# Two stages of a software pipeline, each cut in two: the divisors of the attention contexts and the running products of the cosines

## The chip, the cores and the metric

The kernel runs on one core of one Trainium2 chip. The time is device microseconds (us) of one launch, taken as the median of several runs. The times of single instructions come from the trace of one profiled execution.

## What is computed

Four layers work on four images of 128 channels and 64 x 64 pixels. A state-space layer and a convolution come first (layers 0 and 1), then an attention with a small feed-forward (layer 2), an expert layer, a linear attention, and an expert layer again. The change lies in layer 2. There an image is 4096 tokens of 128 numbers, in 16 heads of 8; the queries, keys and values of a head are one and the same tensor, made of running products of cosines:

```python
def _qz_ring(phi):
    c = jnp.cos(phi)
    P = jnp.cumprod(c, axis=-1)
    z0 = jnp.prod(c[..., 1:], axis=-1, keepdims=True)
    return jnp.concatenate([z0, P[..., 1:]], axis=-1)
...
qkv = _qz_ring(heads + rx_theta)
...
attn = jax.nn.softmax(scores, axis=-1)
ctx = jnp.einsum('bhst,bhtd->bhsd', attn, q)
...
x1 = _ln(x + attn_out, g1, beta1)
zf = jnp.cos(x1[..., :NQ_FFN]) * jnp.cos(ry_theta)
h = jax.nn.relu(zf @ w1.T + b1)
ffn_out = h @ w2.T + b2
return _ln(x1 + ffn_out, g2, beta2)
```

The input of the layer is a layernorm of the tokens, and its answer is added to them.

## The kernel before

Layer 2 (`layer2_attention`, L825) takes the images one after another, in a loop over `b` at L1312 that runs five times. Each pass has two stretches. In the first one, `prepare` of image `b` (L914) and `feed_forward` of image `b - 1` (L1227) run side by side; in the second, `attention` of image `b` runs (L1003). So the first pass holds preparation alone, the next three hold both (called joint stretches here), and the fifth holds feed-forward alone. The attention has the order of PE, DVE and POOL written out by hand (`manual_schedule`) and is not touched.

An image is cut into eight chunks of 512 tokens. A stage is a function of the chunk's number `c`, and `in_turn` (L797) makes a pipeline of stages: in turn `i` it calls stage `k` for chunk `i - k`, the last stage first. `run` (L820) takes the steps of several such pipelines by turns, one call of each. What these calls record is not yet the order on the engines. Outside the attention a scheduler of the compiler takes all recorded instructions, with their dependencies and buffers, and lays them out engine by engine, in an order that depends on its own estimate of when each can start. On the chip each engine then works through its list in order, and an instruction that has to wait holds up all behind it on that engine. Loads and stores are issued on SP, in order as well.

Preparation has five stages. `fetch` loads the chunk (`x_in`). `centred` subtracts the mean on PE (`ln_xc`) and squares on ACT (`ln_sq`). `norm` makes the variance on PE (`ln_var`), the inverse root on DVE and ACT (L110 to L115) and the normed chunk on DVE (`nrm`, L118), which is stored. `products` turns the chunk to tokens on PE (`tok_t`, L943), adds the angle on DVE (`phi`, L945), and takes the cosine, `K.cos` (L196): the multiple of two pi on DVE and ACT (`cos_k`, L200 and L201), the rest on DVE (`cos_r`, L203 and L204), the absolute value and the sine on ACT (L205, L206), each sine after a table load where the last table was that of the square root. The result is `cs`. Still in `products`, POOL multiplies the cosines 1 to 7 (`q0`, one L955 and five L957), DVE makes seven running products in place (L959), the first of which overwrites what POOL reads, and DVE copies `q0` into place 0 (L960). `store` copies `cs` to the values on ACT (L965), every second time starts four stores of them, turns it on PE (`q_t`, L980), copies that (`tq`, ACT), splits it in two parts on DVE and POOL (`rest`, `part`, L984 to L987) and stores these as heads (L988). At the end the first head's keys and queries are loaded back (L903, 32 loads) and rounded on POOL (L912).

Feed-forward has nine stages. `fetch` loads the two halves of the contexts (`num`, two buffers), the sums of their weights (`den`) and the normed chunk (`nrm_in`). `attended` turns the sums on PE (`den_t`, L1246), adds them up and takes the reciprocal on DVE (L1248 to L1250), copies it for the 8 numbers of each head (`rc`, L1252), turns it back on PE (`rd_ps`), adds the halves on POOL (L1256), divides on DVE (L1257), multiplies with a weight on PE (`att_ps`) and adds to the normed chunk on DVE (L1260). Then come `first_centred` and `first_norm` (a layernorm that ends on POOL, L121), `cosines` (`z_ps`, then `K.cos` as `zf`), `hidden` (`hid_ps`, four relus on ACT), `sum_up` (`ffn_ps`, L1295), `last_centred`, and `last_norm`, which adds to the tokens on POOL (L1306) and stores them (L1307).

PE is the matrix engine, DVE the vector engine, ACT the engine of activations, POOL the general one, SP the queue of loads and stores.

Of the kernel before, what the change touches and what calls it, by code (L numbers as in the profile page):

```python
# [9 lines left out]
F32 = mybir.dt.float32  # L10
# [7 lines left out]
P = 128  # L18
# [4 lines left out]
NCH = L // CH  # L23
# [773 lines left out]
def in_turn(n, *stages):  # L797


    for i in range(n + len(stages) - 1):  # L800
        for k in reversed(range(len(stages))):
            if 0 <= i - k < n:
                stages[k](i - k)
                yield
# [20 lines left out]
def layer2_attention(K, xd, dpool, w):  # L825

    nc, tc, mm = K.nc, K.tc, K.mm
    NH, HD = 16, 8
# [3 lines left out]
    with ExitStack() as ctx:  # L832
# [77 lines left out]
        def rounded(t):  # L910

            nc.gpsimd.tensor_copy(t, t.bitcast(F32))  # L912

        def prepare(b, big, two, work, psum):  # L914

            n = NTT * NH * (HD + 1)
            qt = big.tile([P, n + 32], F32, name="qt")
            nc.gpsimd.memset(qt[:, n:], 0.0)  # L920
            values = qt[:, 0:n].rearrange("p (h t d) -> p t h d", h=NH, d=HD + 1)
            nc.gpsimd.memset(values[:, :, :, HD : HD + 1], 1.0)
            shape = [P, 4, NH, HD]
            heads, xs, nrms, laters, halves = {}, {}, {}, {}, {}

            def fetch(c):
                xs[c] = work.tile([P, CH], F32, name="x_in", bufs=3)
                nc.sync.dma_start(out=xs[c], in_=xd[b][:, c * CH : (c + 1) * CH])

            def centred(c):  # L930
                nrms[c] = work.tile([P, CH], F32, name="nrm", bufs=3)
                halves[c] = K.layernorm_steps(nrms[c], xs.pop(c), work, psum, tag="xc", bufs=3)
                next(halves[c])

            def norm(c):
                next(halves.pop(c), None)
                nc.sync.dma_start(out=nrm_d[b % 2][:, c * CH : (c + 1) * CH], in_=nrms[c])

            def products(c):

                tp = psum.tile([P, 4, P], F32, name="tok_t", tag="mm")
                for j in range(4):
                    nc.tensor.transpose(tp[:, j, :], nrms[c][:, j * P : (j + 1) * P], K.ident)  # L943
                phi = work.tile(shape, F32, name="phi")
                nc.vector.tensor_tensor(  # L945
                    phi.rearrange("p t h d -> p (t h) d"),
                    tp.rearrange("p j (h d) -> p (j h) d", d=HD),
                    theta.unsqueeze(1).to_broadcast([P, 4 * NH, HD]),
                    ALU.add,
                )  # L950
                cs = heads[c] = work.tile(shape, F32, name="cs", bufs=3)
                K.cos(cs, phi, work, shape, "cos")
                cc = lambda d: cs[:, :, :, d : d + 1].rearrange("p t h o -> p (t h) o")
                q0 = work.tile([P, 4 * NH, 1], F32, name="q0")
                nc.gpsimd.tensor_tensor(q0, cc(1), cc(2), ALU.mult)  # L955
                for d in range(3, HD):
                    nc.gpsimd.tensor_tensor(q0, q0, cc(d), ALU.mult)  # L957
                for d in range(1, HD):
                    nc.vector.tensor_tensor(cc(d), cc(d - 1), cc(d), ALU.mult)  # L959
                nc.vector.tensor_copy(cc(0), q0)  # L960

            def store(c):

                cs = heads[c]
                nc.scalar.copy(values[:, 4 * c : 4 * c + 4, :, 0:HD], cs)  # L965
                j = c // 2
                if c % 2 == 0 and j < NJ - 1:
                    laters[j] = work.tile([P, NH, BT, HD], F32, name="later", bufs=1)
                if j < NJ - 1:
                    at = laters[j][:, :, 4 * (c % 2) : 4 * (c % 2) + 4]  # L970
                    nc.gpsimd.tensor_copy(at.rearrange("p h t d -> p t h d"), cs)
                if c % 2 and j < NJ - 1:
                    for q in range(4):
                        nc.sync.dma_start(
                            out=value_d[:, :, j, q].rearrange("h s t d -> s h (t d)"),
                            in_=laters[j][32 * q : 32 * q + 32].rearrange("s h t d -> s h (t d)"),
                        )
                tp = psum.tile([P, 4, P], F32, name="q_t", tag="mm")
                for j in range(4):
                    nc.tensor.transpose(tp[:, j, :], cs[:, j].rearrange("p h d -> p (h d)"), K.ident)  # L980
                tq = work.tile([P, CH], F32, name="tq", tag="phi")
                nc.scalar.copy(tq, tp.rearrange("p j t -> p (j t)"))
                rest = work.tile([P, CH], F32, name="rest", tag="cos_r")
                nc.vector.scalar_tensor_tensor(rest, tq, 4097.0, tq, ALU.mult, ALU.subtract)  # L984
                part = work.tile([P, 2, CH], F32, name="part")
                nc.vector.scalar_tensor_tensor(part[:, 0], tq, 4097.0, rest, ALU.mult, ALU.subtract)
                nc.gpsimd.tensor_tensor(part[:, 1], tq, part[:, 0], ALU.subtract)  # L987
                nc.sync.dma_start(  # L988
                    out=head_d[:, :, c * CH : (c + 1) * CH].rearrange("z q s -> q z s"), in_=part
                )  # L990

            first = []

            def stages():
                yield from in_turn(NCH, fetch, centred, norm, products, store)
                first.extend(load(0, two))
                for t in first:
                    rounded(t)
                yield

            return stages(), qt, first

        def attention(qt, first, dsum, big, two, work, pssc, psctx, psacc):  # L1003
# [222 lines left out]

        def feed_forward(b, dsum, work, psum):  # L1227

            loads, x1s, hids, sums, halves, lasts = {}, {}, {}, {}, {}, {}

            def fetch(c):
                cols = slice(c * CH, (c + 1) * CH)
# [5 lines left out]
                nc.sync.dma_start(out=nrm, in_=nrm_d[b % 2][:, cols])  # L1238
                loads[c] = num, den, nrm

            def attended(c):
                num, den, at = loads[c]

                tp = psum.tile([P, 4, 2 * NH], F32, name="den_t", tag="mm")
# [3 lines left out]
                nc.vector.tensor_reduce(rd, tp.rearrange("p j (z h) -> p j h z", z=2), AX.X, ALU.add)  # L1248
                nc.vector.tensor_tensor(rd, rd, dsum[:, 4 * c : 4 * c + 4], ALU.add)
                nc.vector.reciprocal(rd, rd)  # L1250
                rc = work.tile([P, 4, NH, HD], F32, name="rc")
                nc.vector.tensor_copy(rc, rd.unsqueeze(3).to_broadcast([P, 4, NH, HD]))  # L1252
                rp = psum.tile([P, 4, P], F32, name="rd_ps", tag="mm")
                for j in range(4):
                    mm(rp[:, j, :], rc[:, j].rearrange("p h d -> p (h d)"), K.ident)
# [46 lines left out]
            def last_norm(c):  # L1302
# [3 lines left out]
                nc.gpsimd.tensor_tensor(x, x, o, ALU.add)  # L1306
                nc.sync.dma_start(out=xd[b][:, c * CH : (c + 1) * CH], in_=x)  # L1307

            return in_turn(NCH, fetch, attended, first_centred, first_norm, cosines, hidden, sum_up, last_centred, last_norm)

        past = None
        for b in range(NB + 1):  # L1312
# [459 lines left out]
```

## Time and profile before

| | us |
|---|---|
| median of 3 runs | 10838.9 (10834.5 to 10853.2) |
| profiled execution | 10849.6 |
| its span, first to last instruction | 10847.5 |
| preparation alone (3204.0 to 3357.8) | 153.8 |
| three joint stretches, last exponential of one image to first of the next | 247.8, 248.7, 249.1 |
| feed-forward alone (9536.7 to 9689.6) | 152.9 |
| busy in the span: PE, DVE, ACT, POOL | 9021, 7648, 7513, 5239 |

The five stretches are some 1052 us of the span; the attention blocks between them take about 1358 us each. In the views below, a line of the timeline has the start in us from the span's start, the duration, the engine, the line of the program, the operation, what it writes and reads with shapes, and in brackets how long the engine stood idle before it and what ended that. A row of the table of busy time has a stretch, its length, and for each engine the busy time and the number of instructions in it. A row of the waits says which engine's operation waited for which, then total, number of times and longest.

### The profile page before, as it was taken

The numbers are of one execution on the slowest core, as the hardware profiler recorded it, in microseconds if no ns is written. First come the engines' busy times: TensorE is split into PE (matmuls) and PEld (weight loads), VectorE is DVE, ScalarE is ACT, GpSimd is POOL, SyncE is SP. The second block draws the span as 40 slices with busy tenths as digits, with TensorE's granted clock in tenths as the row PEclk, the third lists the DMA queues.
The fourth block names the chain that finished last, engine by engine and source line by source line (L and its number), as shares of the span: only waits on it lengthen the run. The fifth ranks groups of instructions, "written<-read, shape, count | busy, mean of one in ns | idle before, by whom it ended". The sixth has DMA issues, their size and how long they took to land. (4 is left out here: it accounts for less than half of the span.)

```text
span 10847.5 us, 184105 instructions
## 1 busy us (share of the span) xinstructions
PE 9021.2 (83%) x71952; PEld 3473.1 (32%) x71952; DVE 7647.7 (71%) x8462; ACT 7513.2 (69%) x10317; POOL 5239.0 (48%) x3143
## 2 busy tenths in 40 slices
PE   5777778777866999978999978999978999976767
PEld 2123323322342333333333333333333333323433
DVE  2787677668856777767777767777767777754563
ACT  2665575565526999967999968999958999942431
POOL 1565555556634655645566635666635665520000
PEclk8788878878878999989999989999989999987888
DMA  3322322321212112222221122222222212223004
GB/s 81 88 70 56 89 73 55 86 75 50 62 60 49 34 33 36 37 68 44 33 38 35 33 71 42 38 35 34 33 75 42 35 34 33 33 89 105 6 17 140
DMA packets 524325, 581.58 MB, mean 54 GB/s; under 512 B 106232, under 2 KB 329536, under 8 KB 520896
## 3 DMA queue, kind: packets, MB, share of 16 engines
q1 hardware_dynamic: 523456, 569.81, 22.9%
q8 instruction: 568, 9.31, 0.4%
q14 instruction: 301, 2.47, 0.1%
HBM read 373.96 MB, written 76.55 MB: 42 GB/s over the span
## 5 line engine op out<-in xcount | busy, mean ns | idle before, releaser
L1208 ACT ACTIVATE ex<-score 128x1024 f32<-128x1024 f32 x5120 | 4934.2, 1033 | 469.8 <-PE score L90 180.1
L90 PE MATMUL ctx_ps<-ex,qt 128*32 128x512 f32 x20480 | 2719.4, 595 | 0.0
L1155 POOL TENSOR_TENSOR folded<-ex 128x1024 f32<-128x1024 f32 x704 | 1679.6, 2386 | 2074.2 <-ACT ex L1208 2054.2
L1214 DVE STREAM_TRANSPOSE turned<-ex 128x1024 f32<-128x1024 f32 x1536 | 1879.5, 1224 | 491.5 <-ACT ex L1208 428.1
L90 PE MATMUL acc_ps<-turned,turned_v 128*32 128x256 f32 x24576 | 1826.2, 388 | 181.4 <-DVE turned L1194 179.6
L1194 DVE STREAM_TRANSPOSE turned<-ex 128x1024 f32<-128x1024 f32 x1536 | 1854.0, 1207 | 0.0
L90 PE MATMUL score<-queries,keys 32*128 32x512 f32 x10240 | 1358.3, 496 | 140.7 <-ACT ex L1208 81.0
L687 DVE TENSOR_TENSOR_SCAN hs<-decay,carry,hs 128x512 f32<-128x512 f32 x1024 | 1252.8, 1266 | 197.3 <-ACT decay L686 183.0
L686 ACT ACTIVATE decay<-dt,a_neg 128x512 f32<-128x512 f32 x1024 | 700.9, 689 | 794.3 <-DVE hs L687 772.6
L90 PEld LDWEIGHTS score<-queries,keys 32*128 32x128 f32 x10240 | 524.3, 182 | 2196.0 <-issue 1666.2
L693 POOL TENSOR_TENSOR hs<-hs,c_sb 128x1024 f32<-128x1024 f32 x512 | 1205.1, 2375 | 43.5 <-DMA c_sb<-c_d 24.0
L1156 POOL TENSOR_TENSOR quarters<-folded 128x512 f32<-128x512 f32 x704 | 905.4, 1286 | 55.2
L90 PEld LDWEIGHTS acc_ps<-turned,turned_v 128*32 128x32 f32 x24576 | 561.6, 108 | 897.8 <-issue 555.8
L90 PEld LDWEIGHTS ctx_ps<-ex,qt 128*32 128x32 f32 x20480 | 684.5, 109 | 461.4 <-DVE ctx L1137 53.1
L90 PE MATMUL y_ps<-hs,pair 128*64 128x512 f32 x2048 | 652.3, 761 | 138.6 <-POOL hs L693 138.5
L683 DVE TENSOR_TENSOR hs<-dtx,b_ps 128x2048 f32<-128x2048 f32 x256 | 582.3, 2275 | 261.8 <-PE b_ps L90 177.1
L1137 DVE COPY ctx<-ctx_ps 128x512 f32<-128x512 f32 x256 | 177.0, 692 | 669.8 <-PE ctx_ps L90 669.8
L690 POOL COPY carry<-hs 128x4 f32<-128x4 f32 x256 | 59.8, 234 | 1028.0 <-DVE hs L687 990.5
L1027 POOL TENSOR_TENSOR turned_v<-v,quarter 128x1024 f32<-128x1024 f32 x192 | 459.5, 2394 | 17.4 <-ACT ex L1208 11.1
L1201 DVE TENSOR_REDUCE dacc<-quarters 128x2 f32<-128x512 f32 x704 | 453.2, 644 | 7.2 <-POOL quarters L1156 7.2
L90 PE MATMUL b_ps<-dbc,spread 32*128 32x512 f32 x512 | 322.3, 712 | 64.5 <-DVE hs L683 64.4
L1208 ACT ACTIVATION_READ_ACCUMULATOR ex<-score 128x1 f32 x1664 | 348.7, 210 | 0.0
(353 smaller groups left out, 9574.1 us busy)
## 6 DMA issues: line engine op xcount, KB each, us to landing
c_sb<-c_d SPq DMA_DIRECT2D x512, 128.0 KB
queries<-head_d SPq DMA_DIRECT2D x1024, 64.0 KB
keys<-head_d SPq DMA_DIRECT2D x1024, 64.0 KB
dt<-dt SPq DMA_DIRECT2D x128, 256.0 KB
dtx<-dtx SPq DMA_DIRECT2D x128, 256.0 KB
w<-in_L_ffn_weight SPq DMA_DIRECT2D x32, 1024.0 KB
w<-in_L_ffn_weight SPq DMA_DIRECT2D x128, 256.0 KB
under<-xp SPq DMA_DIRECT2D x384, 66.0 KB
```

What stands on the lines that cost most here:

```text
L90: self.nc.tensor.matmul(out, lhsT, rhs, start=start, stop=stop)
L683: nc.vector.tensor_tensor(hs, dtx2, bb.unsqueeze(1).to_broadcast([P, NQ, CH]), ALU.mult)
L686: nc.scalar.activation(ex, dt2[:, q, :], AF.Exp, scale=a_neg[:, q, g : g + 1])
L687: nc.vector.tensor_tensor_scan(hs[:, q, :], ex, hs[:, q, :], carry[:, g, q : q + 1], ALU.mult, ALU.add)
L693: nc.gpsimd.tensor_tensor(at, at, cs.unsqueeze(1).to_broadcast([P, 2, CH]), ALU.mult)
L1027: nc.gpsimd.tensor_tensor(t, v.unsqueeze(2).to_broadcast([P, 4 * BT, 4, HD]), quarter.unsqueeze(1).to_broadcast([P, 4 * BT, 4, HD]), ALU.mult,
L1155: nc.gpsimd.tensor_tensor(hs, exs[:, :, 0], exs[:, :, 1], ALU.add)
L1156: nc.gpsimd.tensor_tensor(qs, hs[:, :, 0 : CH // 2], hs[:, :, CH // 2 :], ALU.add)
L1194: nc.vector.transpose(*upright)
L1201: nc.vector.tensor_reduce(at, qs, AX.X, ALU.add)
L1208: nc.scalar.activation(ex, sps[p], AF.Exp, scale=scale, accum_out=dacc[:, j, h, t : t + 1] if summed else None)
L1214: nc.vector.transpose(*upright)
```

## The change

The stage `products` of preparation ends with the cosine, and what followed it becomes a stage of its own, `running`. The stage `attended` of feed-forward gives its first half, up to `rc`, to a stage `divisors`; `rc` is handed on in a dictionary. Preparation has six stages then and feed-forward ten. No instruction is added or taken away in the program text, and no buffer count is changed.

```diff
                 cs = heads[c] = work.tile(shape, F32, name="cs", bufs=3)
                 K.cos(cs, phi, work, shape, "cos")
+
+            def running(c):
+                cs = heads[c]
                 cc = lambda d: cs[:, :, :, d : d + 1].rearrange("p t h o -> p (t h) o")
                 q0 = work.tile([P, 4 * NH, 1], F32, name="q0")
...
-                yield from in_turn(NCH, fetch, centred, norm, products, store)
+                yield from in_turn(NCH, fetch, centred, norm, products, running, store)
...
-            loads, x1s, hids, sums, halves, lasts = {}, {}, {}, {}, {}, {}
+            loads, x1s, hids, sums, halves, lasts, rcs = {}, {}, {}, {}, {}, {}, {}
...
-            def attended(c):
+            def divisors(c):
                 num, den, at = loads[c]
...
-                rc = work.tile([P, 4, NH, HD], F32, name="rc")
+                rc = rcs[c] = work.tile([P, 4, NH, HD], F32, name="rc")
                 nc.vector.tensor_copy(rc, rd.unsqueeze(3).to_broadcast([P, 4, NH, HD]))
+
+            def attended(c):
+                num, _, at = loads[c]
+                rc = rcs.pop(c)
                 rp = psum.tile([P, 4, P], F32, name="rd_ps", tag="mm")
...
-            return in_turn(NCH, fetch, attended, first_centred, first_norm, cosines, hidden, sum_up, last_centred, last_norm)
+            return in_turn(NCH, fetch, divisors, attended, first_centred, first_norm, cosines, hidden, sum_up, last_centred, last_norm)
```

Built, the two programs differ in the order of their instructions in the five stretches, and in nothing else but two more table loads on ACT in each joint stretch. One turn on DVE in preparation alone, in the middle of the stretch (the number is that of the chunk, the lines are those of before):

```
before: phi 4, rest 3, cos_k 4 (L200), part 3, ln_vt 5 (L110), cos_r 4 (L203), cos_r 4 (L204),
        inverse root 5 (L113, L115), nrm 5 (L118), products 4 (4 x L959), q0 4 (L960), products 4 (3 x L959)
after:  phi 4, rest 2, product 3, part 2, product 3, q0 3 (L960), cos_k 4 (L200), product 3, ln_vt 5 (L110),
        2 products 3, cos_r 4 (L203), product 3, cos_r 4 (L204), product 3, inverse root 5, nrm 5 (L118)
```

In a joint stretch the products of one chunk are laid in the same way between the steps of the next chunk's cosine and those of feed-forward.

## The prediction

> **What bounds the kernel now.** I read the page's first table, then the table of busy time by stretch for the five stretches that the change touches, then two stretches of the timeline and the table of waits. The page shows no engine at its limit over the whole span: PE 83%, DVE 71%, ACT 69%. The change touches nothing in the attention blocks, so the question is what limits the stretches between them: preparation alone, three stretches in which preparation and feed-forward share the engines, and feed-forward alone.
>
> ```profile
> core 0: us, PE busy (x) PEld busy (x) DVE busy (x) ACT busy (x) POOL busy (x), PEclk, DMA share, GB/s
> 3204.00:3357.80 153.80, 41.84 (x102) 20.87 (x102) 68.42 (x148) 54.91 (x76) 38.22 (x66) 0.56 0.32 84
> 4715.30:4963.10 247.80, 154.79 (x446) 72.29 (x442) 149.09 (x290) 116.08 (x172) 84.68 (x99) 0.76 0.34 95
> ...
> 9536.70:9689.60 152.90, 113.14 (x344) 49.45 (x340) 83.88 (x146) 69.96 (x105) 45.77 (x32) 0.84 0.31 99
> 4723.00:4893.00 170.00, 105.37 (x293) 51.51 (x293) 108.57 (x226) 79.84 (x119) 53.20 (x77) 0.73 0.33 104
> ```
>
> In no row does an engine pass 75%. In the part of a joint stretch where both jobs run (last row) DVE, the busiest, works 108.6 of 170 us. These stretches wait on chains of dependent instructions. The chain of preparation stands in the timeline, from one cosine (`cs`) to the next:
>
> ```profile
> 3248.40 0.72 ACT L206 ACTIVATE cs<-cos_r,half_pi 128x512 f32<-128x512 f32 x1
> 3249.20 0.30 POOL L955 TENSOR_TENSOR q<-cs 128x64 f32<-128x64 f32 x1 [4.05 <-ACT cs L206]
> ...
> 3249.57 2.16 POOL L957 TENSOR_TENSOR q<-q,cs 128x64 f32<-128x64 f32 x5
> ...
> 3251.77 0.23 DVE L960 COPY cs<-q 128x64 f32<-128x64 f32 x1 [0.76 <-POOL q L957]
> 3251.88 0.89 DVE L959 TENSOR_TENSOR cs<-cs 128x64 f32<-128x64 f32 x3
> ...
> 3253.79 1.06 PE L943 MATMUL tok_t<-ident,nrm 128*128 128x128 f32 x4
> ...
> 3254.89 0.69 DVE L945 TENSOR_TENSOR phi<-tok_t,theta 128x512 f32<-128x512 f32 x1 [2.12 <-PE tok_t L943]
> ...
> 3257.66 1.39 DVE L203 SCALAR_TENSOR_TENSOR cos_r<-cos_k,phi 128x512 f32<-128x512 f32 x1
> ...
> 3262.05 0.72 ACT L206 ACTIVATE cs<-cos_r,half_pi 128x512 f32<-128x512 f32 x1
> ```
>
> One chunk's cosine waits for the whole product of the chunk before: `tok_t` of the next chunk stands behind `q_t` on PE, and `q_t` waits for the last product on DVE. The eight cosines start from 3221.7 to 3313.1, so a turn is 91.4/7 = 13.06 us. In the first joint stretch they start from 4747.0 to 4884.1: 137.1/7 = 19.6 us. In feed-forward the waits name the divisors:
>
> ```profile
> PE rd_ps L90 <- DVE rc L1252: 13.8, 6, 3.6
> ```
>
> This is the last stretch (9536 to 9690): PE, in order, stands 13.8 us ahead of the broadcast of the divisors while `den_t`, four DVE steps and back follow one another.
>
> **What the Trainium skill says.** ScalarE: Activation LUTs, What ACT_TABLE_LOAD costs, gives 1283 ns a load and a drain beside it; the trace agrees on 1283 ns, and the next ACT instruction starts 1.29 us after the load, with no drain to be seen. GPSIMD Engine Reference, Specifications, says that GpSimd and VectorE contend for an SBUF interface when the DVE instruction has two SBUF inputs; the trace agrees: L203 above takes 1.39 us beside a POOL operation, 0.69 at 3218.2 without one. TensorE: Matmul & The Clock Gate, part 1, says an idle PE falls to half clock; here eight `rd_ps` records span 2.08 us at 9546.9, after a long idle stretch, and 1.13 at 9588.4.
>
> **The change part by part.** It adds no arithmetic and no DMA. Built, both programs have the same instructions on PE, DVE, POOL and SP; ACT gets two more table loads in each joint stretch, 6 x 1.283 = 7.7 us. ACT is busy 116 of 248 us there, so I take 0; uncovered, they cost 7.7.
>
> *Products in preparation.* In the new order `tok_t`, `phi` and `cos_k` of chunk c+1 no longer stand behind the seven products of chunk c; these are laid between the DVE steps of the next cosine. I follow the order from the end of cosine c, with the durations above. POOL's six products end at 2.6 (0.08 + 2.5); the copy of q0 at 2.85, `cos_k` on DVE (0.42) at 3.3, where ACT takes over (0.72). DVE goes on with one product, a transpose (0.71), two products, L203 (0.69), a product and L204 (0.63), to 6.4 with starts 0.05 to 0.08 closer than the durations. ACT: absolute value 0.63 to 7.0, the copy `qt` 0.66, table load 1.28, cosine 0.72: 9.7. POOL's `part` will hold up one DVE step (the 1.39 against 0.69): 10.2. The turn goes from 13.06 to 10.2, seven turns: 20.0 us. The end of the stretch (last head store, 32 loads issued on SP, roundings) starts earlier by as much and is not shortened. -20.
>
> *Both parts in the joint stretches.* Cosine 6 to cosine 7 in the new order, from L203 to L203: L203, transpose, L204, then ACT's absolute value, one relu, load, cosine (end at 5.3), POOL's first product to 5.65, for which DVE idles 2.3 us ahead of its first product; then 20 DVE steps of together 10.0, starting 0.05 closer, none of which waits by this reckoning: 14.7. Cosine 3 to 4: 32 DVE steps of together 16.7, less 1.6 for the starts, and 1.1 of waits for `att_ps` and `ln_var`: 16.2. Mean 15.5, and 1.0 for DVE steps that collide with POOL (about one a turn is stretched in the trace of before, too): 16.5 against 19.6, seven turns: 22. After the last `q_t`, chunk 8's divisors used to come late: `att_ps` followed that `q_t` (4888.6) by 11.4 us (4900.0), of which 2.8 were PE's wait for `rc`; in the new order it stands behind `tq`, three chains of DVE steps and `num`, some 6. So 5 more. 27 a stretch, 81 in three. What is late next is DVE itself: its busy 108.6 us is the floor for the 165 us between the first `den_t` and the last `q_t`.
>
> Queues passed: on SP the loads of `num` now stand two turns ahead of their use, each waiting for `att_ps` of two chunks before; behind them stand loads of later chunks, and stores of `nrm` and `part`, which have a turn to spare. On POOL, `part` now follows the next chunk's six products (2.5 us later); only the head stores wait for it. New on DVE: a product of chunk c that waits for POOL holds up feed-forward steps queued behind it, the 2.3 us counted above. Buffers: `cs` has three, and three chunks are now alive; `num`, two; I take 0, since the third-last chunk's readers are a turn old.
>
> *Divisors in the last stretch.* `rd_ps` now finds `rc` ready. The 13.8 us go; against it, `num` stands behind `zf_r` on DVE, so `att_ps` follows `z_ps` by 0.69 + 0.72 + 0.69 + 0.65 + 0.69 and gaps = 3.7, under which PE has `ln_var`, `ln_xc` and `rd_ps`, 3.1: 0.6 lost, at most the 0.88 that is lost there now. The stores and loads that follow wait for the last addition at 9689.6 and move with it. -14.
>
> Sum: 20 + 81 + 14 = 115. Profiled execution: 10849.6 (span 10847.5, 2.1 around it) - 115 = 10734.6. The median, 10838.9, lies 10.7 lower; carried over: 10724.
>
> **The rivals.** *Only the unmixed stretches gain.* DVE is in order, and small products that wait for POOL now stand ahead of feed-forward steps; if each turn's waits fill what the turn saves, the joint stretches give 0 to 10 each. For it: the 2.3 us, and DVE work that does not shrink: 149 us in a joint stretch, about what the two single ones hold (68.4 + 83.9). Against it: the walked turns are shorter even with it. 20 + 14 + 15 = 49, half of each at the least: 10790, from 10760 to 10815.
>
> *Slower: a longer pipeline of turns that are no shorter.* Preparation goes from 12 to 13 turns, feed-forward from 16 to 17. If what sets a turn is not the product or the divisor but the rest of the chain, each stretch costs one more turn: 13.1 + 3 x 19.6 + 14 = 86, 10925. It decides where the joint turn stays over 12/13 of 19.6 = 18.1 us. For it: the first joint turns hold the loads of `den` and `num`. Against it: in the built order nothing after the last cosine is moved back; the turns are not walls.
>
> *Larger gain.* If latency were all hidden, DVE's floor would give 165 - 108.6 = 56; realistically 40 a stretch with a warmer PE: 20 + 120 + 18 = 158: 10681.
>
> *The change does nothing:* excluded as to order, which is moved; that a gain in one stretch is lost before the next is possible only where DMA ends it, but in the joint stretches the first `ex` waits for the last store of feed-forward.
>
> **How the numbers follow.** Main forecast 0.58 (10695 to 10760), partial gain 0.18, larger gain 0.06, slower 0.13, within 0.2% (21.7 us, about what can be told from no change) 0.05 as the poor end of the partial case. The range leaves out the slower case and half of the no-change case, and reaches to the larger gain: 10675 to 10815. Faster 0.82, same 0.05, slower 0.13.
>
> **What would show it.** Right: in preparation alone the cosines start 10 us apart, and 16 to 17 in the joint stretches; `PE rd_ps <- DVE rc` is gone from the waits; a joint stretch, last `ex` to first, falls from 248 to near 221; its DVE busy time stays near 149. Wrong: cosines still 19 us apart with DVE waiting on POOL `q` or ACT, or more stretched DVE steps (busy over 160), or a stretch ended by another wait after 4893's counterpart, such as the SP queue's head loads.

## The result and the profile after

| | before | after |
|---|---|---|
| median, us | 10846.1 (4 runs, 10834.5 to 10855.0) | 10709.4 (4 runs, 10708.6 to 10709.5) |
| profiled execution, us | 10849.6 | 10709.5 |
| its span, us | 10847.5 | 10707.7 |
| ahead of the attention layer (start of its first step, L200 `ry_k`) | 3203.9 | 3189.7 |
| preparation alone, from `ry_k` to the first exponential | 153.8 | 140.9 |
| three joint stretches | 247.8, 248.7, 249.1 | 215.8, 217.0, 216.0 |
| four attention blocks together | 5433.2 | 5432.5 |
| feed-forward alone, to its last store | 153.0 | 137.8 |
| behind that store | 1157.9 | 1157.9 |

The ratio is 0.9875, interval 0.9863 to 0.9886: the changed kernel is faster by 1.25%, 136.6 us between the medians. The two profiles differ by 139.8 us. Of these, 14.2 lie ahead of the attention layer, where both programs are the same; 12.9 lie in preparation alone, 96.8 in the joint stretches, 15.2 in feed-forward alone and 0.7 in the attention blocks. So what the change itself gave in these profiles is 125.6 us.

The table of busy time for three of the five stretches, in the changed kernel (columns as in the prediction):

```profile
core 0: us, PE busy (x) PEld busy (x) DVE busy (x) ACT busy (x) POOL busy (x), PEclk, DMA share, GB/s
3190.00:3330.70 140.70, 40.86 (x102) 20.36 (x102) 70.78 (x147) 53.33 (x76) 41.47 (x66) 0.61 0.37 92
4687.70:4903.50 215.80, 139.23 (x446) 64.26 (x442) 150.49 (x290) 118.44 (x176) 85.48 (x99) 0.83 0.38 109
9412.00:9550.00 138.00, 107.37 (x344) 47.09 (x340) 85.21 (x146) 69.79 (x106) 45.42 (x32) 0.86 0.35 109
```

The work is what it was: DVE 150.5 us in the joint stretch (149.1 before), ACT 2.4 us more for its two table loads. Only PE needs less time for the same 446 matmuls, 139.2 us for 154.8, at a granted clock of 0.83 for 0.76; no edit here separates this from the shorter waits. For the rest, what went away is idle time. DVE stood idle for 98.7 us of a joint stretch before (247.8 - 149.1) and stands idle for 65.3 now.

The chain of one turn of preparation in the changed kernel's timeline, from one cosine to the next:

```profile
3237.07 0.72 ACT L206 ACTIVATE cs<-cos_r,half_pi 128x512 f32<-128x512 f32 x1
3237.51 0.69 DVE L945 TENSOR_TENSOR phi<-tok_t,theta 128x512 f32<-128x512 f32 x1 [1.21 <-PE tok_t L943]
...
3239.07 0.42 DVE L962 TENSOR_TENSOR cs<-cs 128x64 f32<-128x64 f32 x1
...
3244.10 0.67 DVE L203 SCALAR_TENSOR_TENSOR cos_r<-cos_k,phi 128x512 f32<-128x512 f32 x1
3244.69 0.26 DVE L962 TENSOR_TENSOR cs<-cs 128x64 f32<-128x64 f32 x1
3244.88 0.68 DVE L204 SCALAR_TENSOR_TENSOR cos_r<-cos_k,cos_r 128x512 f32<-128x512 f32 x1
...
3246.20 1.09 PE L983 MATMUL q_t<-ident,cs 128*128 128x128 f32 x4 [5.31 <-DVE cs L962]
...
3248.14 0.72 ACT L206 ACTIVATE cs<-cos_r,half_pi 128x512 f32<-128x512 f32 x1
```

The next chunk's angle (`phi`) follows 0.4 us behind the start of this chunk's cosine, where it used to stand behind all of its products. The products (L962) lie between the steps of the next cosine. The eight cosines run from 3207.3 to 3279.2, 72.0/7 = 10.3 us a turn (13.06 before). In the first joint stretch they run from 4714.9 to 4827.6, 112.8/7 = 16.1 us a turn (19.6 before).

### The profile page after: what moved, and what is told of

It is laid out like the page before. It is cut to its first block, busy times and chain, and to the rows that moved or that the text cites. A ratio compares the mean times of both kernels' runs of the same rounds, so it can differ in the third digit from the quotient of the medians.

```text
span 10707.7 us, 184050 instructions
## 1 busy us (share of the span) xinstructions
PE 8939.2 (83%) x71952; PEld 3434.1 (32%) x71952; DVE 7658.7 (72%) x8462; ACT 7518.8 (70%) x10323; POOL 5247.7 (49%) x3143
## 5 line engine op out<-in xcount | busy, mean ns | idle before, releaser
L90 PEld LDWEIGHTS ctx_ps<-ex,qt 128*32 128x32 f32 x20480 | 683.8, 109 | 461.6 <-DVE ctx L1140 53.3
L683 DVE TENSOR_TENSOR hs<-dtx,b_ps 128x2048 f32<-128x2048 f32 x256 | 582.6, 2276 | 248.5 <-PE b_ps L90 167.1
```

The costliest lines, as they stand in the source:

```text
L90: self.nc.tensor.matmul(out, lhsT, rhs, start=start, stop=stop)
L683: nc.vector.tensor_tensor(hs, dtx2, bb.unsqueeze(1).to_broadcast([P, NQ, CH]), ALU.mult)
```

## The experiments

Every kernel has a profile of its own. The times of the stretches in it, each worked out from the starts in its timeline, as in the table above (the joint stretch is the mean of three):

| kernel | median | `ry_k` starts | preparation alone | joint stretch | feed-forward alone | whole layer |
|---|---|---|---|---|---|---|
| before | 10846.1 | 3203.9 | 153.8 | 248.5 | 153.0 | 6485.6 |
| before, again | 10840.7 | 3194.0 | 156.4 | 249.1 | 150.2 | 6486.2 |
| after | 10709.4 | 3189.7 | 140.9 | 216.3 | 137.8 | 6360.0 |
| running only | 10729.2 | 3199.6 | 144.6 | 215.2 | 160.8 | 6383.5 |
| divisors only | 10755.8 | 3207.5 | 154.2 | 224.9 | 136.3 | 6397.8 |
| x with 4, den with 2 | 10700.4 | 3185.9 | 139.0 | 215.7 | 135.9 | 6353.9 |
| x with 4, den with 3 | 10698.2 | 3197.0 | 139.1 | 214.3 | 134.3 | 6349.3 |
| after without `rest` | 10694.2 | 3192.5 | 130.8 | 212.7 | 137.9 | 6338.9 |
| before without `rest` | 10819.3 | 3202.2 | 151.4 | 241.4 | 154.5 | 6462.4 |
| three for two | 10775.3 | 3205.3 | 140.9 | 238.0 | 133.0 | 6421.3 |
| five for four | 10722.2 | 3195.0 | 137.9 | 216.8 | 138.0 | 6359.4 |
| early queries | 10716.6 | 3200.2 | 143.3 | 216.6 | 134.0 | 6359.4 |
| merged | 10714.8 | 3195.1 | 139.2 | 212.3 | 148.1 | 6359.5 |
| merged in part | 10703.7 | 3192.9 | 140.2 | 213.3 | 134.3 | 6348.9 |

The whole layer, from `ry_k` to its last store, is the measure that the rest of the program doesn't disturb.

**The kernel before, once more.** No edit.

> The kernel before, unchanged, profiled once more. After the change the first instruction of the attention layer (L200, ry_k) starts at 3189.7 us; it was 3203.9 in the profile of the kernel before, 14.2 us that lie ahead of everything the change touches. Theory A (these 14.2 us are the scatter of one execution to another in the first two layers): here the same instruction starts elsewhere than 3203.9, by several us, and the spread of the medians is of that size. Theory B (the changed program moves the first two layers too): here it starts within 1 us of 3203.9, and ratio 1.000 within 0.05%. Both: the five stretches of the attention layer last what they lasted, 153.8, 247.8, 248.7, 249.1 and 152.9, within 1 us.

The row of that step in its timeline:

```profile
3193.96 0.15 DVE L200 TENSOR_SCALAR ry_k<-ry 128x1 f32<-128x1 f32 x1 [9.29 <-DMA ry<-in_L_attn_ry_theta]
```

The same program reaches the attention layer 10.0 us earlier than in its other profile, while its layer lasts 6486.2 us against 6485.6. Over the 14 profiles `ry_k` starts between 3185.9 and 3207.5 in no order that follows the edits. So theory A holds: the 14.2 us ahead of the layer are scatter of the first two layers. The expectation that the five stretches repeat within 1 us was wrong: the joint ones here last 248.4, 245.9 and 252.9, preparation alone 2.6 us more and feed-forward alone 2.8 us less than in the other profile, and that the layer's total agrees within 0.6 us is partly luck. The length goes with the clock that PE was granted: 0.75, 0.77 and 0.74 in these three joint stretches. So a difference of 4 us between single stretches is not read below. Against this second profile of before, the gains of the change would be 15.5 in preparation alone, 98.4 in the joint stretches and 12.4 in feed-forward alone. The medians agree: ratio 1.0, interval 0.9991 to 1.0008.

**One part alone: the products.** The edits from here on are against the changed kernel.

```diff
-            def divisors(c):
+            def attended(c):
...
-            def attended(c):
-                num, _, at = loads[c]
-                rc = rcs.pop(c)
...
-            return in_turn(NCH, fetch, divisors, attended, first_centred, first_norm, cosines, hidden, sum_up, last_centred, last_norm)
+            return in_turn(NCH, fetch, attended, first_centred, first_norm, cosines, hidden, sum_up, last_centred, last_norm)
```

> Only the running products are a stage of their own; the divisors stay where they were. Theory A (the two parts add up, each in its own chain): preparation alone as in the changed kernel, 140.9 us from ry_k to the first exponential (before 153.9); feed-forward alone as before; a joint stretch 248 - 22 = 226. Total 13 + 66 = 79 less than before. Theory B (in a joint stretch the divisors' wait on PE takes the place of the products' one, so that one part alone gives little): joint stretches 240 or more. Theory C (the products are nearly all of it in a joint stretch): 218 or less.

**One part alone: the divisors.**

```diff
-            def running(c):
-                cs = heads[c]
...
-                yield from in_turn(NCH, fetch, centred, norm, products, running, store)
+                yield from in_turn(NCH, fetch, centred, norm, products, store)
```

> Only the divisors are a stage of their own; the products stay behind the cosine. Theory A (the two parts add up): preparation alone as before, 153.9; feed-forward alone 15 us shorter; a joint stretch about 10 shorter (4.6 ahead of the first cosine, 5 behind the last), 238, its cosines 19 to 20 us apart as before. Total 45 less than before. Theory B (one part alone gives little): joint stretches 245 or more, total 15 to 25 less. Theory C (the divisors make most of a joint stretch's gain): 228 or less.

The ratios are 0.9893 (0.9879 to 0.9906) for the products and 0.9919 (0.9906 to 0.9933) for the divisors. Outside the joint stretches each part shortens its own lone stretch and not the other, as theory A has it. Its number for feed-forward alone fails with the products only: 160.8 where 153.0 was expected. The order there is the old one; its first `zf` comes 5.8 us later than before, its last one 99.7 us after the first (97.8 before). The four profiles with that order last 150.2, 153.0, 154.5 and 160.8 us at granted clocks of 0.86, 0.84, 0.83 and 0.82, so this is scatter that goes with the clock. In the joint stretches theories A and B are wrong in both runs. The products alone give 33 us, the divisors alone 24, and both together 32. They don't add, and it isn't that one alone gives little: either alone gives most of it. Both numbers of theory C came true (under 218 and under 228), but the two can't both be the explanation.

The two parts also gain in other places than expected. The run with the divisors was to leave the cosines 19 to 20 us apart; they are 16.4 apart there, nearly as in the changed kernel, and 17.5 with the products alone. With the products alone it is the time from the last cosine to the first exponential that falls, from 79.1 to 60.2 us. Where a gain shows depends on where the steps of feed-forward were laid: in the first joint stretch 260 of PE's matmuls lie between the first cosine and the last with the products alone, 200 with the divisors alone.

Why the divisors speed up preparation is seen before the change, in the longest turn of the first joint stretch, from 4801.6 to 4830.4 us:

```profile
4814.68 2.08 PE L90 MATMUL rd_ps<-ident,rc 128*128 128x128 f32 x8 [0.24 <-DVE rc L1252]
...
4817.53 2.08 PE L90 MATMUL att_ps<-num,w_comb 128*128 128x512 f32 x2 [0.78 <-DVE num L1257]
...
4819.40 1.06 PE L943 MATMUL tok_t<-ident,nrm 128*128 128x128 f32 x4
```

The `nrm` that this `tok_t` turns was ready at 4807.0. It stands 12.4 us behind two `ln_xc` of feed-forward, the `q_t` of the chunk before, `den_t`, `rd_ps` and `att_ps` on PE, while the divisors are made on DVE. Over the eight chunks of the first joint stretch `tok_t` starts 71.9 us in all after its `nrm` has ended; with the products alone it is 52.9, with the divisors alone 51.3, with both 16.2, and the other two joint stretches agree within 4 us. This wait is what both parts take away, and here they do more than add (19.0, 20.6 and 55.7 us). The stretch does not follow in full. With both parts the rest of a turn lies in other steps: in those that make `nrm`, which `tok_t` now follows closely, and in those from `tok_t` to the cosine, which take 82.4 us over the eight chunks for 72.1 before.

One thing that grows in exchange is seen in the group of the products (line, engine, operation, number; busy time, mean ns of one; idle time ahead of them). Before:

```profile
L959 DVE TENSOR_TENSOR cs<-cs 128x64 f32<-128x64 f32 x56 | 16.9, 301 | 12.5 <-POOL q L955 10.7
```

With the products alone as a stage, first joint stretch:

```profile
L962 DVE TENSOR_TENSOR cs<-cs 128x64 f32<-128x64 f32 x56 | 18.5, 331 | 6.5 <-POOL q L958 4.8
```

And in the changed kernel:

```profile
L962 DVE TENSOR_TENSOR cs<-cs 128x64 f32<-128x64 f32 x56 | 23.0, 411 | 2.2 <-POOL q L958 1.3
```

The wait for POOL goes from 12.5 to 6.5 to 2.2 us, but the same 56 products take 16.9, 18.5 and 23.0 us. Their median is 275 ns, the longest 1385. I compared each DVE step of the stretch with the shortest one of its kind: 12 steps were over 0.2 us longer before (8.2 us in all), 11 with the products alone (6.6), 22 in the changed kernel (14.2). Each of them lies beside an operation of POOL, which only 118 of the 290 steps do in the changed kernel. The Trainium skill, GPSIMD Engine Reference, Specifications, names the contention of the two engines for an SBUF interface for DVE instructions with two SBUF inputs, which the products are. So from the products alone to both, DVE's products wait 4.3 us less and take 4.5 us longer. Part of the second gain can be lost there; no edit tested it, and it doesn't show that nothing else holds the stretch at 215.

**Is DVE the bound now?** The step `rest` is left out.

```diff
-                rest = work.tile([P, CH], F32, name="rest", tag="cos_r")
-                nc.vector.scalar_tensor_tensor(rest, tq, 4097.0, tq, ALU.mult, ALU.subtract)
...
-                nc.vector.scalar_tensor_tensor(part[:, 0], tq, 4097.0, rest, ALU.mult, ALU.subtract)
+                nc.vector.scalar_tensor_tensor(part[:, 0], tq, 4097.0, tq, ALU.mult, ALU.subtract)
```

> The changed kernel without the DVE step rest of every chunk (L987, 0.69 us); the first part of a head is formed from tq itself, so its splitting in two parts is left out. The step lies on no chain from one cosine to the next. In the seven turns of a joint stretch DVE is now busy 95.7 of 112.7 us. Theory A (DVE is what bounds the turns of the changed kernel): a joint stretch loses 7 or 8 times 0.69, some 5 us, 15 in three. Theory B (chains and PE's order still bound the turns): under 1.5 us a stretch. Preparation alone, DVE 70.8 of 140.9 us: under 2 us in both.

The same edit in the kernel before:

> The same step left out of the kernel before, where DVE is busy 88.6 of 137.1 us in the seven turns. There rest stands behind q_t and ahead of the next chunk's cosine steps. Theory A (before the change chains set the turns, after it DVE): a joint stretch loses under 2 us here. Theory B (DVE's work set the turns before the change, too): 5 us a stretch.

A joint stretch of the changed kernel loses 3.6 us for 8 x 0.69 = 5.5 us of DVE work, one of the kernel before 7.1 (against 248.5). That is between the theories for after, and theory A is wrong for before. Preparation alone loses 10 us in the changed kernel, not under 2: its eight cosines span 66.3 us for 72.0, and its tail, which scatters by that much, is 46.7 for 51.4. The expectation that `rest` lies on no chain was wrong, and DVE's share of 85% in the turns of the changed kernel is not shown to be a new bound. The most direct reading is that DVE's in-order queue is part of the turn in both kernels. But the edit does not take away 0.69 us of DVE time alone: it also frees the buffer that `rest` shares with `cos_r`, and the order on DVE changes (the products of the first joint stretch take 19.2 us and wait 4.8, for 23.0 and 2.2). These were not separated.

**The mixture.** Stages of feed-forward recorded for stages of preparation, three for two:

```diff
-                    run(*parts)
+                    if len(parts) == 2:
+                        in_pace(parts[0], 3, parts[1], 2)
+                    else:
+                        run(*parts)
```

`in_pace` calls so many steps of the one and then so many of the other until both have ended.

> The changed kernel with another mixture in the joint stretches: three stages of feed-forward are recorded for two of preparation (one for one before). In the changed kernel preparation's last head is stored 64 us ahead of the first exponential, though loads and roundings behind it took 48 us where nothing else ran; in the seven turns DVE is 85% busy, and in the 46 us after them PE 88%. Theory A (the two parts are unevenly mixed, so that first DVE and then PE is the bound): a joint stretch falls from 216 to 200 to 208, 25 to 45 us in three. Theory B (the sum of DVE's work and its waits sets the stretch, whatever the order): 213 to 219. Theory C (feed-forward's steps ahead delay preparation, whose loads then end the stretch): over 222.

And five for four:

> The changed kernel with five stages of feed-forward recorded for four of preparation in the joint stretches. At three for two the stretch lasted 238: preparation's cosines were 21 us apart, and the last cosine was followed by 56 us of products, stores, loads and roundings; at one for one preparation ends 18 us earlier than it would have to. Theory A (the best mixture lies between, and little depends on the exact ratio): cosines over 118 to 125 us, the stretch 206 to 213. Theory B (any call of feed-forward ahead of preparation makes its turns longer by as much as it frees at the end): 216 to 225, the tail from the last cosine to the first exponential falling as the cosines grow.

Three for two is theory C: 238 us, with DVE at 144.7 us of the 239.2 of its first stretch. The cosines last 147 us instead of 113, with more of feed-forward's steps recorded ahead of preparation's; the last cosine is then followed by 56 us of products, stores, loads and roundings. Five for four gives 216.8: cosines over 127 us, 57 us behind them, theory B. What is gained behind the last cosine (19 us) is lost ahead of the first one (5) and in the turns (15).

**The end of the joint stretch.** The POOL rows at the end of the first one, in the changed kernel:

```profile
4890.91 1.56 POOL L121 TENSOR_SCALAR blk<-ln_rs,beta 128x512 f32<-128x512 f32 x1
4892.44 1.26 POOL L1313 TENSOR_TENSOR x<-x,blk 128x512 f32<-128x512 f32 x1
4898.46 1.26 POOL L1313 TENSOR_TENSOR x<-x,blk 128x512 f32<-128x512 f32 x1 [4.76 <-issue]
```

The last addition starts 6.0 us after the one before it, though its `blk` was ready. The view names nothing that ended the wait ("issue"); the load of its `x` was issued at 4894.8.

```diff
-                x = loads[c] = work.tile([P, CH], F32, name="x", bufs=3)
+                x = loads[c] = work.tile([P, CH], F32, name="x", bufs=4)
...
-                den = work.tile([2 * NH, CH], F32, name="den", bufs=3)
+                den = work.tile([2 * NH, CH], F32, name="den", bufs=2)
```

> The changed kernel with four buffers for the tile x of the final addition (three before), and two for den (three before), so that it fits. Theory A: in the changed kernel a joint stretch ends on the loads of x: the last one is issued at 4894.8, behind three stores on SP, the last addition follows at 4898.5 where blk was ready at 4892.5, and the first exponential at 4903.5. With a fourth buffer the last addition follows blk, and each joint stretch loses 5 us, feed-forward alone 0 to 5: 15 to 20 less than the changed kernel. Theory B (what ends the stretch is the queue of head loads and stores on SP, or POOL's casts, and a buffer doesn't move it): within 3 us a stretch, total within 10. If the third buffer of den mattered, the cosines of a joint stretch drift apart by more than 17 us.

With three buffers for `den`, and one for each of `rd` and `q0` instead:

> The changed kernel with four buffers for x as before, but with the third buffer of den kept; rd and q0, small tiles, get one buffer each, so that it fits. With two buffers for den the tail of a joint stretch, from the last zf to the first exponential, fell from 30.1 to some 26.3, while its head and its cosines grew by 3.4 together. Theory A (den's lost buffer ate the gain): joint stretches of 212 to 213.5. Theory B (what the tail gains is lost ahead of it whatever den has, through x loads that stand in SP's queue earlier): 215 to 217.

The wait ahead of the last addition goes, and the time from the last `zf` to the first exponential falls from 30.1 to 26.3 in both. But the stretch is 215.7 in the first (theory B) and 214.3 in the second, 2 us less than after and between its two theories: the lost buffer of `den` accounts for 1.4 us at most. In both, POOL's two roundings of the heads (L912, 3.8 us) stand right ahead of the last three additions. The ratio of the second is 0.986 (0.9846 to 0.9875), not to be told from the changed kernel's.

**The tail of preparation alone.** Eight loads of queries moved (`load_part` issues the loads of one kind and of the given half; the loads at the end are cut to match):

```diff
             def store(c):
 
+                if c == NCH - 1:
+                    first.extend(two.tile([P, L // 2], F32R, name=name) for name in ("keys", "queries"))
+                    load_part(0, first, False, (0,))
                 cs = heads[c]
```

> The changed kernel with eight of the loads of queries, those that need no token of the last chunk, recorded ahead of the last chunk's store. Built, 8 loads instead of 1 stand ahead of the last head store on SP in preparation alone, and 24 instead of 31 behind it. Theory A (the tail of preparation alone is SP's issue of loads, 0.72 to 0.96 us each): the 51.4 us from the last cosine to the first exponential become 45, the stretch 135 instead of 140.9. Theory B (the tail is the data's way, not the issue): within 2 us. Joint stretches within 3 us in both, since their last store is one of feed-forward.

This experiment says nothing on the tail, and its expectation was wrong on what was built: in preparation alone the scheduler laid the eight loads behind the last head store all the same (38 loads of heads ahead of the first exponential, as in the changed kernel); only in the joint stretches they moved, where nothing changed (216.6), as both theories had it.

**Divisors without the longer pipeline.**

```diff
             def first_centred(c):
+                attended(c)
...
-            return in_turn(NCH, fetch, divisors, attended, first_centred, first_norm, cosines, hidden, sum_up, last_centred, last_norm)
+            return in_turn(NCH, fetch, divisors, first_centred, first_norm, cosines, hidden, sum_up, last_centred, last_norm)
```

> The changed kernel with attended and first_centred as one stage: divisors stay a stage of their own, and feed-forward has nine stages and 16 turns again. In a joint stretch the divisors alone gain 24 us, the products alone 32, and both together only 32. Theory A (the divisors' stage gives back what it gains through its extra turn): the first zf comes 53.3 us after the last exponential in the changed kernel and 45.3 with the products alone, 8 us; with nine stages it comes at 46, and a joint stretch lasts 208 to 212. Theory B (the products and the divisors remove the same waits, of PE's queue in a turn, and the extra turn costs nothing): 214 to 219. Theory C (the stage's two halves, att_ps and ln_xc, wait for each other on PE in one turn): 220 or more. Feed-forward alone shows the same: A 2 to 4 us less than the changed kernel, C 5 to 10 more.

The first `zf` comes at 43.7 us (53.3 in the changed kernel), as theory A has it; the stretch falls by 4.0 on average (214.6, 208.6, 213.8), just short of A's range and at the edge of what such stretches scatter (the 208.6 has a granted clock of 0.87, the others 0.83). In feed-forward alone it is theory C: 10.3 us more, with turns of up to 16 us. So the extra turn may cost something, but over half of the some 10 us by which the first `zf` comes earlier is lost again later in the stretch. Theory B's reason, that products and divisors remove the same waits on PE, is not what the waits of `tok_t` above show.

Both findings together, merged in the joint stretches only, with four buffers for `x`:

```diff
+            def both(c):
+                attended(c)
+                first_centred(c)
+
+            heads = [attended, first_centred] if b == NB - 1 else [both]
-            return in_turn(NCH, fetch, divisors, attended, first_centred, first_norm, cosines, hidden, sum_up, last_centred, last_norm)
+            return in_turn(NCH, fetch, divisors, *heads, first_norm, cosines, hidden, sum_up, last_centred, last_norm)
```

> Attended and first_centred as one stage in the joint stretches, where that gave 214.6, 208.6 and 213.8 us against 215.8, 217.0 and 216.0 of the changed kernel, and two stages in feed-forward alone, where one stage cost 10 us; x with four buffers, rd and q0 with one. If both add: joint stretches of 209 to 212, feed-forward alone as changed (last store at 134 to 138 us), 12 to 20 us less than the changed kernel, some 10693. If the joint stretches have a floor that no order of these stages passes (DVE's 150 us beside a head and a tail of together some 57): 212 to 215, 5 to 12 less than the changed kernel, near 10700.

Joint stretches of 214.1, 213.8 and 211.9: the second alternative. The layer is 11 us shorter than in the changed kernel, the median is 10703.7 us, and its interval (0.986 to 0.9893) covers the changed kernel's. By the medians no version here beats it by more than can be told; by the layer's time, in one profile each, this one and four buffers for `x` with three for `den` do by 11 us.

## Why the prediction was right, and where its terms were not

**The sum.** Predicted: 20 + 81 + 14 = 115 us in the layer. Measured in the profiles: 12.9 + 96.8 + 15.2, and 0.7 in the attention blocks, 125.6. The remaining 14.2 of the profiled difference are scatter ahead of the layer, which nothing in the argument could give. The likeliest case was the one that came, and its time, 10724, lies 15 us above the median. Luck has a part in this. Preparation alone was put 7 us too high and the joint stretches 16 too low, and these partly cancel to the 11 that the terms were off. The 14.2 of scatter would have added to that, but the 10.7 that the forecast took off to come from the profile to the median were not there after the change (10709.5 and 10709.4), so the two nearly cancel as well.

**Preparation alone: the turns right, the tail wrong.** The walk gave 10.2 us a turn and 20.0 for seven; measured are 10.3 and 91.4 - 72.0 = 19.4. The sentence that the end of the stretch "starts earlier by as much and is not shortened" failed: it became longer, 51.4 us from the last cosine to the first exponential for 44.7. The last head store comes 11.0 us after the last cosine (9.15 before), because two chunks' products and heads now end together, and 38 loads stand behind it on SP for 36. At 0.83 us for one (13 loads in 10.8 us before) these two terms make 3.5. The rest is scatter: the nine profiles with the products as a stage (`rest` in place) have tails of 44.9 to 51.9, mean 49.6; the three with the old order 44.7 to 45.9. The edit meant to separate issue from transfer here did not reach the place, so why the loads take longer is open.

**The joint stretches: the mis-sized term.** 27 a stretch was the forecast, 32.3 the result (means of three):

| | forecast | before | after | gain |
|---|---|---|---|---|
| last exponential to first cosine | 0 | 32.8 | 27.7 | 5.1 |
| seven turns | 22 | 136.7 | 112.7 | 24.0 |
| last cosine to first exponential | 5 | 79.1 | 75.9 | 3.2 |

The head of the stretch was taken as unmoved, and that was the largest error, 15 us in three stretches. In the timeline of before, rows ahead of the first cosine:

```profile
4735.79 0.69 DVE L118 TENSOR_TENSOR nrm<-ln_xc,ln_rs 128x512 f32<-128x512 f32 x1
...
4737.13 1.12 PE L90 MATMUL att_ps<-num,w_comb 128*128 128x512 f32 x2 [1.00 <-DVE num L1257]
...
4738.95 0.60 PE L943 MATMUL tok_t<-ident,nrm 128*128 128x128 f32 x4
...
4742.68 0.68 DVE L203 SCALAR_TENSOR_TENSOR cos_r<-cos_k,phi 128x512 f32<-128x512 f32 x1
```

And after:

```profile
4708.03 0.69 DVE L118 TENSOR_TENSOR nrm<-ln_xc,ln_rs 128x512 f32<-128x512 f32 x1
...
4708.87 0.63 PE L943 MATMUL tok_t<-ident,nrm 128*128 128x128 f32 x4 [1.74 <-DVE nrm L118]
...
4711.34 1.12 PE L90 MATMUL att_ps<-num,w_comb 128*128 128x512 f32 x2
4711.48 0.69 DVE L203 SCALAR_TENSOR_TENSOR cos_r<-cos_k,phi 128x512 f32<-128x512 f32 x1 [0.19 <-ACT cos_k L201]
```

The step that makes the normed chunk starts 20 us behind the last exponential in both. Before, its `tok_t` stood behind the second chunk's `att_ps` on PE, and its cosine steps behind a layernorm of feed-forward on DVE: 6.9 us from `nrm` to L203. After, `tok_t` comes first, and it is 3.5 us. The experiments tie this to the divisors: the head is 27.2 to 29.2 with the divisors alone, 31.0 to 34.5 with the products alone (31.0 to 35.0 in the two profiles of before).

In the turns the total was near, but its parts were not. Two of the seven turns were walked, from L203 to L203. The one from cosine 6 to 7 took 17.5 us where the walk gave 14.7 (without collisions), the one from 3 to 4 took 16.6 for 16.2. In the first, DVE was to wait for POOL ahead of its first product and for nothing after. The wait is another one:

```profile
4800.43 0.69 DVE L200 TENSOR_SCALAR zf_k<-z_ps 128x512 f32<-128x512 f32 x1 [4.30 <-PE z_ps L90]
```

A step of feed-forward stands ahead of the first product on DVE and waits for its own matmul. In all, DVE is idle for 17.0 us of the seven turns (95.7 busy of 112.7), 2.4 a turn, so the 2.3 was right in size and wrong in place: all 56 products of a stretch wait 2.2 us, and the waits are ahead of `zf_k` (5.5), of the copies of `q0` (5.7) and of others. Against that, the collisions with POOL were put at 1.0 us a turn; the steps that are stretched cost 14.2 us in the stretch, 1.8 a chunk. That the seven turns still came to 16.1 each, near the 16.5 of the sum, is due to the other five, which were not walked and took 15.6 on average. This is luck in part. So is the 19.6 that was set against it: it is a mean over turns of 14.5 to 28.8 us, and 14 of the 24 us come from the longest turn, the one shown above, which became 14.6. DVE's busy time stayed at 150.5, as forecast, because more steps follow at once and overlap a little: their durations add up to 166.1 us (161.1 before). PE's waits behave as foretold: `rd_ps` behind `rc` 1.7 us in the stretch for 10.4, `q_t` behind the products 7.4 for 20.5. The two table loads came (29 for 27); no edit tested whether they are hidden.

The tail: `att_ps` of the last chunk follows the last `q_t` by 6.0 us, as forecast (11.4 before). But that `q_t` itself comes 1.7 us later behind its cosine, so that 3.7 of the 5 are left.

What the prediction did not see is that the two parts overlap. It made one walk over both, so its sum does not depend on it, but a reader who takes 22 for the one and 5 for the other is wrong: either part alone brings 24 to 33, and the divisors alone bring 22 in the turns. All versions with the products as a stage lie between 212 and 217 us, except three for two. What holds them there is not settled: DVE's queue (3.6 us back for 5.5 taken away) and its collisions with POOL may be part of it.

**Feed-forward alone: right in sum, not in its parts.** The waits of PE in the last stretch of the changed kernel:

```profile
PE att_ps L90 <- ACT zf_r L205: 5.1, 4, 1.6
PE att_ps L90 <- DVE num L1264: 4.5, 4, 2.0
PE rd_ps L90 <- DVE rc L1255: 3.2, 2, 1.7
```

The 13.8 us ahead of `rd_ps` became 3.2, not zero: two waits are left. The loss ahead of `att_ps` was put at 0.6 a chunk and no more than the 0.88 of before; the group waits 9.7 us for 6.0 before, 3.7 more. All of PE's waits together fell from 33.5 to 24.4. The other 5.8 are PE's own: 107.4 us busy for 113.1 with the same 344 matmuls, 315 ns for 354 in `rd_ps`, at a granted clock of 0.86 for 0.84. That agrees with what the Trainium skill says in TensorE: Matmul & The Clock Gate, part 1, of an idle PE, but no edit tested it alone. A faster PE was left to the rival of a larger gain; it belonged in this sum. With the scatter of this stretch the match of 14 and 15.2 is partly luck: the nine profiles with both stages apart or the divisors alone last 133.0 to 138.0, mean 135.7, the four of the old order 150.2 to 160.8, mean 154.6, which makes 19.

**The rivals.** Slower through longer pipelines: the cost is real, since the first `zf` comes at 53.3 us in the changed kernel and at 45.3 with the products alone, but a turn of 16.1 lies well under the 18.1 at which it would decide. A joint stretch that gains little: wrong, since waits for POOL did not take the saved time. The larger gain: 32.3 us a stretch lie about halfway between the 27 of the forecast and the 40 of this rival.

## What to carry to other kernels

Where two pipelines share in-order engines, ask what each instruction of the one stands behind in the other: here a chain of divisors in feed-forward held up preparation on PE as much as preparation's own products did. Look at the head of the stretch, too: a split that makes one pipeline wait less moves the other one's first steps forward on every queue that they share. Gains of two splits that act on the same stretch are not to be added; cost them together, or one after the other on the order that the first leaves. When small steps move in between other work, charge them for collisions with the engine that they now run beside, and expect an added stage to lengthen the end where several chunks finish at once (here 1.9 us to the last head store). Walk more turns than two where their lengths differ by a factor of two.

## What was not expected of the hardware

The parts of the program that the edits don't touch differ from profile to profile by up to 33 us (4334 to 4367 us of the span outside the attention layer), while the attention layer of the same kernel repeats within 0.6 us in the two profiles of before, though its single stretches move by up to 4 us. A DVE product of 128x64 numbers takes 275 ns in the median and up to 1385 beside a POOL operation. The same 446 matmuls of a joint stretch took 139 to 160 us of PE. The order explains only part of that: in two stretches of the second profile of before, with one order, they took 153.9 us at a granted clock of 0.77 and 159.6 at 0.74. A load of 64 KB takes 0.83 us of SP's time on average in one profile and 0.96 in another (15 loads in 14.4 us), at the same place in the program.
